# One load of the weight instead of two, held in slots, with eight mean subtractions moved to GpSimd and the rounding of the weight ranked lower, in a layernorm + banded product + fp8 linear kernel

## The chip, the cores and the metric

The kernel runs on one core of one Trainium2 chip. The metric is the time of one execution on the device, in microseconds (us). The kernel before takes 323.88 us (median of 3 runs, 323.79 to 323.97). Engines are named as in the profile: PE is TensorE (PEld its weight loads), DVE is VectorE, ACT is ScalarE, POOL is GpSimd, SP is SyncE, which issues most loads.

## The reference, cut to what matters

x is 4096 rows (8 x 512) of 1024 float32.

```
xn   = layernorm(x)                            # per row, no scale and shift
attn = einsum('ds,td->st', w1, w2) * sparse_mask
y    = gelu(xn @ attn + b2)
w_q  = fp8_e4m3(weight * (448 / max|weight|))
x_q  = fp8_e5m2(xn * (57344 / max|xn|))
z    = (x_q @ w_q.T) / x_scale / w_scale + bias
out  = x + y + z
```

Two numbers are maxima over everything: max|weight| and max|xn|. No fp8 product can start before both are known, and max|xn| needs every row of x to be normalized (or its mean taken off, and the maximum multiplied by the row's inverse deviation).

## The kernel before, in words

The rows are 32 tiles of 128 x 1024. Tiles 0 to 15 are "early": they stay in SBUF from their first load. Tiles 16 to 31 are "late": they are loaded for their statistics and maximum, dropped, and loaded again for the linear stage. sparse_mask is zero outside a band, so each 128-row piece of attn is multiplied on at most 268 columns (`band`, `band_pieces`); a check at the end, `check_mask`, looks at the rest and sets a flag, on which a general path would run.

First stage. `load_attn` brings w1, the columns of w2 and the mask for each of the eight pieces of attn (L248), `attn_matmuls` and `attn_mask` form them. For an early tile: `statistics` (DVE, L292), a root of variance for a group of tiles (`GROUPS`, by GpSimd in `inverse_root_gpsimd`, L337, for all but the first and last group), `normalize` on ScalarE for tiles 0 and 1 and `normalize_gpsimd` (L375) for the others, `row_max` (DVE, L380), eight transposes on TensorE (`transpose_one`, L462), two evictions (ScalarE, or VectorE for the second half of tiles 8 to 15), a preload of b2 into PSUM (`preload`, L483), the banded product (`product_matmul`, L487) and gelu (L497). For a late tile: tiles 16 to 23 have mean and squares taken by ScalarE (`mean_of`, `squares`), tiles 24 to 31 have statistics by VectorE and their mean taken off by ScalarE (`mean_minus`, L313); then `row_max_late` (L385).

The weight is loaded twice by `load_weight` (L257): once for its row maxima (`weight_amax`, L428), and once more to be scaled by ScalarE (`weight_scaled`, L433), given a rounding constant by VectorE (`weight_magic`, L437, two buffers), and rounded by GpSimd in two halves of two instructions each (`weight_rounded`, L446). The maxima over all rows go through two tiny transposes on TensorE (`amax_rows` to `scale_and_inverse`, L390 to L417).

Second stage. `quantize` (L516) makes fp8 tiles; the linear of each tile is interleaved on TensorE with the product of a late tile and the transposes of the next (`interleaved`). GpSimd issues DMAs that add x to the gelu of the early tiles (`add_x`, L500).

The order on every queue is set by `Plan` (L115): each step is written down with an engine, a cost in us, a rank, what it comes after, and what it takes and frees of counted resources (33 slots of 4 KB per partition in the pool "slots", PSUM buffers, "stream", "twice", "magic", "late"). The planner runs these costs forward and each time takes the ready step of lowest rank; the steps are then emitted in that order, and each engine runs its queue in order. Costs and ranks thus move no work by themselves, only its place in the queues. Loads are ranked by their place in `LOADS` (L72).

Of the kernel before, what the change touches and what calls it, by code (L numbers as in the profile page):

```python
# [26 lines left out]
STREAM = 5  # L27
# [3 lines left out]
BY_VECTOR = range(EARLY // 2, EARLY)  # L31
BY_SCALAR = range(0, 2)
GROUPS = [(0, 2), (2, 4), (4, 8), (8, 12), (12, EARLY), (EARLY, EARLY + 8), (EARLY + 8, 28), (28, 32)]
# [37 lines left out]

def load_order():  # L72

    late = iter([*SQUARED, *(i for i in range(EARLY, TILES) if i not in SQUARED)])
    early = iter(range(EARLY))
    found = [("x", next(early)), ("x", next(early))]
    for sc in range(NC):
        found += [("attn", sc)]
        found += [("x", i) for i in (next(early, None), next(early, None)) if i is not None]
        found += [("x", next(late))]  # L80
    found += [("once", c) for c in range(NC)]
    for c in range(NC):
        found += [("twice", c), ("x", next(late))]
    return found
    return found
# [90 lines left out]
def banded_path(  # L176
# [138 lines left out]

    def variance(lo, hi):
        v["var", lo] = small.tile([P, hi - lo], F32, tag="var", name=f"var_{lo}")
        nc.vector.tensor_scalar_add(v["var", lo], mean_var[:, lo:hi, 1], LN_EPS)
# [109 lines left out]
    def weight_amax(c):  # L428
        nc.vector.tensor_reduce(
            w_cols[:, c : c + 1], ws.pop(c), AX.X, ALU.max, apply_absolute_value=True  # L430
        )
# [155 lines left out]
    plan = Plan(slot=SLOTS - 1, quant=QUANT, y=4, f=2, t=2, stream=STREAM, magic=2, twice=4, late=LATE)  # L587
# [6 lines left out]
    def load(cost, emit, *args, take=(), after=()):  # L594
        op = do(LOAD, cost, len(loads), emit, *args, lag=2.0, take=take, after=after)
        loads.append(op)
        return op

    late_first = [i for i in SQUARED]
    late_rest = [i for i in range(EARLY, TILES) if i not in SQUARED]  # L600
    x_ops, attn_ops, w_once, w_twice, mask_ops = {}, {}, {}, {}, {}

    def more(kind, k):
# [4 lines left out]
        elif kind == "once":  # L608
            w_once[k] = load(1.4, load_weight, k, take=("slot", "stream"))
        else:  # L610
            w_twice[k] = load(1.4, load_weight, k, take=("slot", "twice"), after=(w_once[NC - 1],))

    for kind, k in LOADS:
        more(kind, k)

    b2_op = do(G, 0.6, 1, load_b2, lag=12.0, after=(attn_ops[0],))

    attn_mm, attn_ready = [], []
    for sc in range(NC):
        mm = do(  # L620
            T, 3.5, sc * 0.1, attn_matmuls, sc, after=[attn_ops[c] for c in range(sc + 1)],
# [4 lines left out]
            do(V, 0.42, 0, attn_mask, sc, after=(mm,), free=("f",))  # L626
# [5 lines left out]
    for i in range(TILES):  # L632
        if i in SQUARED:
            m = do(A, 1.6, 5 + 0.01 * i, mean_of, i, after=(x_ops[i],))
            stat[i] = do(A, 1.4, 4, squares, i, after=(m,))
        else:
            stat[i] = do(V, 1.43, 4 + 0.01 * i, statistics, i, after=(x_ops[i],))
    for lo, hi in GROUPS:
        group = [stat[i] for i in range(lo, hi)]
        if 0 < lo and hi < TILES:  # L640
            op = do(G, 1.7 + 0.16 * (hi - lo), 0, inverse_root_gpsimd, lo, hi, after=group)
        else:
            op = do(V, 0.2, 0, variance, lo, hi, after=group)
            op = do(G, 0.4 + 0.16 * (hi - lo), 0, power, lo, hi, after=(op,))
# [8 lines left out]
    for i in range(EARLY):  # L653
        if i in BY_SCALAR:
            normal[i] = do(A, 1.14, 3 + 0.01 * i, normalize, i, after=(shifted[i],))
        else:
            normal[i] = do(G, 1.2, 3 + 0.01 * i, normalize_gpsimd, i, after=(shifted[i],))
        maxima[i] = do(V, 1.15, 3 + 0.01 * i, row_max, i, after=(normal[i],))

        settled[i] = do("later", 0.0, i, lambda: None, lag=2.0, after=(normal[i],))  # L660
    for i in range(EARLY, TILES):
        ready = stat[i]
        if i not in SQUARED:
            ready = do(A, 1.14, 3.5, mean_minus, i, after=(ready,))
        maxima[i] = do(V, 1.15, 3 + 0.01 * i, row_max_late, i, after=(ready,), free=("slot", "stream"))
# [9 lines left out]
    def global_amax(name, fp8_max, rank, cols, after):  # L675
# [6 lines left out]
    bias_op = do(G, 0.6, 0, load_bias, lag=6.0, after=(maxima[TILES - 3],), take=("slot",))  # L682

    sums = [
        do(V, 1.15, 2, weight_amax, c, after=(w_once[c],), free=("slot", "stream")) for c in range(NC)
    ]
    w_known = global_amax("w", E4M3_MAX, 0, w_cols, sums)
    rounded = []
    for c in range(NC):
        op = do(A, 1.1, 1, weight_scaled, c, after=(w_known, w_twice[c]))  # L690
        op = do(V, 1.4, 1, weight_magic, c, after=(op,), take=("magic",))
        op = do(G, 2.55, 1, weight_rounded, c, 0, after=(op,))
        rounded.append(do(G, 2.55, 1, weight_rounded, c, 1, after=(op,), free=("slot", "magic", "twice")))
# [5 lines left out]
    for i in range(EARLY):  # L699
        in_big = i >= EARLY - NC  # L700
        for q in range(2):
# [5 lines left out]
            engine, emit = (V, evict_by_vector) if q and i in BY_VECTOR else (A, evict_transposed)  # L707
            evicted[i, q] = do(engine, 0.55, 1.5, emit, i, q, after=(op,), free=("t",))
        pre = [
            do(A, 0.55, 2 + 0.01 * i, preload, i, h, after=(b2_op,), take=("y",)) for h in range(2)  # L710
# [3 lines left out]
        for piece in band_pieces():  # L714
            op = do(
                T, 0.4, 10 * i, product_matmul, i, *piece, lag=0.1 if not piece[-1] else 0.2,
                after=(op, evicted[i, 0], attn_ready[piece[0]], pre[piece[1]]),
            )
            if piece[-1]:
                ends.append(do(A, 0.55, 0, gelu_early, i, piece[1], after=(op, maxima[i]), free=("y",)))  # L720
# [8 lines left out]
    steps = [0]  # L729
    for n in range(1, EARLY):  # L730
# [403 lines left out]
```

## Time and profile before

| what | value |
|---|---|
| median of the runs | 323.88 us |
| time of the profiled execution | 324.16 us |
| its span | 322.3 us |
| mean granted clock of TensorE | 0.987 |
| busy of PE, DVE, ACT, POOL | 290.0, 235.5, 160.9, 136.1 us |
| weight tiles loaded by SP | 16 of 512 KB |
| reads of HBM, writes | 56.60 MB, 16.78 MB |

The profile is of one execution. Starts are us from the start of the span. A row of a timeline gives start, duration, engine, line, operation, output and input, how many records it merges (two records are one float32 matmul), and in brackets how long the engine had been idle and what ended that. The table of stretches gives, for each, the time in which each engine was busy, the mean clock granted to TensorE as a share of full speed, the share of the 16 DMA engines and GB/s.

### The profile page before, as it was taken

How to read it: one execution, taken by the hardware profiler on the slowest of the kernel's cores; microseconds unless marked ns; L12 is line 12 of the kernel's file. 1: busy time of each engine (PE TensorE's matmuls, PEld its weight loads, DVE VectorE, ACT ScalarE, POOL GpSimd, SP SyncE). 2: the span in 40 equal slices, each digit the busy share in tenths (PEclk: the TensorE clock that was granted, in tenths of full speed). 3: DMA queues.
4: the chain of work that ended last, by engine and by line, in shares of the span. 5: the costliest groups of instructions: out<-in, count | busy, mean ns of one | idle time of the engine just before them, and what ended most of it. 6: DMA issues, size and time to landing. Idle time of an engine off the chain costs nothing. (4 is left out here: it accounts for less than half of the span.)

```text
span 322.3 us, 4326 instructions
## 1 busy us (share of the span) xinstructions
PE 290.0 (90%) x1526; PEld 216.9 (67%) x1545; DVE 235.5 (73%) x343; ACT 160.9 (50%) x260; POOL 136.1 (42%) x163
## 2 busy tenths in 40 slices
PE   2669879998899598999989999999999999999992
PEld 0657668887789486876756766676676667667650
DVE  3587797989999899845587677677767766766581
ACT  1467459595895879663244335344523524452110
POOL 2052608183689898996343113311311331131160
PEclk9999999999999789999999999999999999999998
DMA  7999999999607731199999999973344233121313
GB/s 255 399 370 369 380 380 379 373 409 409 254 0 251 272 130 65 11 190 255 293 292 294 305 309 306 410 274 141 120 147 179 72 128 130 75 119 68 132 66 138
DMA packets 28365, 73.74 MB, mean 229 GB/s; under 512 B 3376, under 2 KB 11568, under 8 KB 28336
## 3 DMA queue, kind: packets, MB, share of 16 engines
q1 hardware_dynamic: 20992, 47.17, 40.2%
q0 software_dynamic: 2592, 9.44, 14.2%
q10 hardware_dynamic: 4752, 16.78, 13.1%
q8 instruction: 14, 0.23, 0.3%
q14 instruction: 15, 0.12, 0.1%
HBM read 56.60 MB, written 16.78 MB: 228 GB/s over the span
## 5 line engine op out<-in xcount | busy, mean ns | idle before, releaser
L528 PE MATMUL pf<-wq,xqts 128*128 128x512 bf16 x493 | 145.5, 379 | 1.6 <-DVE x L543 1.0
L488 PE MATMUL py<-attn,xnt 128*128 128x268 f32 (+2 forms) x480 | 115.6, 341 | 2.9 <-ACT py L485 1.7
L488 PEld LDWEIGHTS py<-attn,xnt 128*128 128x128 f32 x480 | 86.3, 190 | 26.3 <-ACT py L485 2.0
L513 POOL TENSOR_TENSOR x<-x,gelu 128x512 f32<-128x512 f32 x32 | 41.2, 1287 | 110.6 <-ACT gelu L510 109.0
L540 DVE SCALAR_TENSOR_TENSOR pf<-pf,descale,bias_bc 128x512 f32<-128x512 f32 x62 | 46.9, 756 | 53.3 <-PE pf L528 50.9
L528 PEld LDWEIGHTS <-xqts 128*128 128x128 fp8e5 x512 | 50.6, 101 | 23.7 <-issue 0.2
L510 ACT ACTIVATE gelu<-py 128x512 f32<-128x512 f32 x32 | 19.1, 597 | 77.7 <-PE py L488 77.7
L543 DVE TENSOR_TENSOR x<-pf,x 128x512 f32<-128x512 f32 x62 | 42.9, 692 | 5.0 <-DMA x<-in_x_dram 1.0
L381 DVE TENSOR_REDUCE row_amax<-x 128x1 f32<-128x1024 f32 x32 | 37.9, 1206 | 6.3 <-POOL x L376 3.0
L278 PE MATMUL pa<-w_sb,w 128*128 128x268 f32 (+1 forms) x128 | 30.5, 393 | 9.6 <-DMA w_sb<-in_w2t_dram 9.5
L488 PE MATMUL py<-attn,xnt_big 128*128 128x198 f32 (+2 forms) x160 | 34.8, 364 | 4.0 <-ACT py L485 4.0
L485 ACT COPY py<-b_bc 128x512 f32<-128x512 f32 x64 | 37.3, 599 | 1.0
L295 DVE BATCH_NORM_STATS2 st<-x 128x6 f32<-128x512 f32 x48 | 30.4, 675 | 9.8 <-DMA x<-in_x_dram 9.8
L478 ACT COPY xnt<-pt 128x512 f32<-128x512 f32 x48 | 27.2, 579 | 15.4 <-PE pt L469 14.8
L278 PEld LDWEIGHTS pa<-w_sb,w 128*128 128x128 f32 x128 | 24.6, 201 | 15.1 <-issue 12.0
L469 PE MATMUL pt<-ident,xn 128*128 128x128 f32 x128 | 34.0, 273 | 0.2
L488 PEld LDWEIGHTS py<-attn,xnt_big 128*128 128x128 f32 x160 | 28.1, 205 | 7.0 <-ACT py L485 4.7
L469 PEld LDWEIGHTS pt<-ident,xn 128*128 128x128 f32 x128 | 17.8, 141 | 14.4 <-DVE xnt_big L481 0.5
L367 ACT ACTIVATE xn<-x,shift,rstd 128x1024 f32<-128x1024 f32 x16 | 19.9, 1244 | 12.0 <-DVE x L543 7.3
L521 DVE TENSOR_SCALAR xqts<-xnt,x_scale 128x1024 fp8e5<-128x1024 f32 x24 | 25.8, 1080 | 0.0
L469 PE MATMUL pt<-ident,x 128*128 128x128 f32 x128 | 19.1, 279 | 3.5 <-ACT xnt L478 1.8
L498 ACT ACTIVATE x<-py 128x512 f32<-128x512 f32 x32 | 18.3, 598 | 6.4 <-PE py L488 6.4
(86 smaller groups left out, 228.1 us busy)
## 6 DMA issues: line engine op xcount, KB each, us to landing
x<-in_x_dram SPq DMA_DIRECT2D x48, 512.0 KB, 8.0
out_dram<-x ACTq DMA_DIRECT2D x31, 512.0 KB, 3.2
w<-in_wt_dram SPq DMA_DIRECT2D x16, 512.0 KB, 8.8
x<-in_x_dram POOLq DMA_DIRECT2D x16, 512.0 KB, 25.5
w<-in_w_dram SPq DMA_DIRECT2D x8, 512.0 KB, 9.4
mask<-in_mask_dram SPq DMA_DIRECT2D x8, 512.0 KB, 9.7
w_sb<-in_w2t_dram SPq DMA_DIRECT2D x6, 512.0 KB, 10.9
attn<-in_mask_dram SPq DMA_DIRECT2D x6, 134.0 KB, 9.5
```

Of the source, the lines that this page charges most:

```text
L278: nc.tensor.matmul(pt[:, : hi - lo], w1_sb[:, c, :], w2_sb[:, c, lo:hi], start=(c == 0), stop=(c == NC - 1),)
L295: nc.vector.bn_stats(st[:, h, :], xs[i][:, half(h)])
L381: nc.vector.tensor_reduce(row_amax[:, i : i + 1], xs[i], AX.X, ALU.max, apply_absolute_value=True)
L469: nc.tensor.transpose(pts[i, q][:, j, :], xn[:, c * P : (c + 1) * P], ident)
L478: nc.scalar.copy(xnts[i][:, q * (NC // 2) : (q + 1) * (NC // 2), :], pts.pop((i, q)))
L485: nc.scalar.copy(pys[i, h], b2_bc[:, half(h)])
L488: nc.tensor.matmul(pys[i, h][:, lo - h * HALF : hi - h * HALF], xnts[i][:, sc, :], attn[:, sc, lo - band(sc)[0] : hi - band(sc)[0]], start ...
L513: nc.gpsimd.tensor_add(xs[i][:, half(h)], xs[i][:, half(h)], gelus[i][:, half(h)])
L521: nc.vector.tensor_scalar(v["quant"][:, xqts[i]], xnts.pop(i), v["x"][0], E5M2_MAX, ALU.mult, ALU.min, saturate=False)
L528: nc.tensor.matmul(v["pf", i, h], v["quant"][:, xqts[i], c, :], wq[:, c, half(h)], start=(c == 0), stop=(c == NC - 1),)
L540: nc.vector.scalar_tensor_tensor(pf, pf, v["descale"], v["bias"][:, half(h)], ALU.mult, ALU.add)
L543: nc.vector.tensor_add(res[:, half(h)], pf, res[:, half(h)])
```

## The change

The weight is loaded once. Its eight tiles stand in the load order behind the fourth of the eight pieces of attn, and keep their slots until the second half of their rounding; `stream` is 8 instead of 5, "twice" is gone. The string `ORDER` gives the loads by kind (a: attn, e: early x, o: weight, s: tiles 16 to 23, l: tiles 24 to 31); late tiles that stood between the early ones now come behind. The means of tiles 24 to 31 are taken off by GpSimd, in one tensor_scalar each. Scaling of the weight has rank 4 instead of 1, its magic 2 instead of 1, its rounding 5 instead of 1. Most costs in the plan are written anew. The order of the second stage is the same.

```diff
-STREAM = 5
+STREAM = 8
+CENTRED_BY_GPSIMD = range(24, 32)
+ORDER = (
+    "eeaeeaeeaeeaooooooooaeeaesaesaesesesesssllllllll"
+)
...
+    def mean_minus_gpsimd(i):
+        nc.gpsimd.tensor_scalar(
+            xs[i], xs[i], -1.0, mean_var[:, i, 0:1], ALU.mult, ALU.add
+        )
...
     def weight_amax(c):
         nc.vector.tensor_reduce(
-            w_cols[:, c : c + 1], ws.pop(c), AX.X, ALU.max, apply_absolute_value=True
+            w_cols[:, c : c + 1], ws[c], AX.X, ALU.max, apply_absolute_value=True
         )
...
-        elif kind == "once":
-            w_once[k] = load(1.4, load_weight, k, take=("slot", "stream"))
         else:
-            w_twice[k] = load(1.4, load_weight, k, take=("slot", "twice"), after=(w_once[NC - 1],))
+            w_ops[k] = load(1.4, load_weight, k, take=("slot",))
...
-        if i not in SQUARED:
-            ready = do(A, 1.14, 3.5, mean_minus, i, after=(ready,))
+        if i in CENTRED_BY_GPSIMD:
+            ready = do(G, 1.23, 4, mean_minus_gpsimd, i, after=(ready,))
+        elif i not in SQUARED:
+            ready = do(A, 1.18, 3.5, mean_minus, i, after=(ready,))
...
     for c in range(NC):
-        op = do(A, 1.1, 1, weight_scaled, c, after=(w_known, w_twice[c]))
-        op = do(V, 1.4, 1, weight_magic, c, after=(op,), take=("magic",))
-        op = do(G, 2.55, 1, weight_rounded, c, 0, after=(op,))
-        rounded.append(do(G, 2.55, 1, weight_rounded, c, 1, after=(op,), free=("slot", "magic", "twice")))
+        op = do(A, 1.17, 4, weight_scaled, c, after=(w_known, w_ops[c]))
+        op = do(V, 1.8, 2, weight_magic, c, after=(op,), take=("magic",))
+        op = do(G, 2.54, 5, weight_rounded, c, 0, after=(op,))
+        rounded.append(
+            do(
+                G, 2.54, 5, weight_rounded, c, 1, after=(op,),
+                free=("slot", "magic"),
+            )
+        )
```

In the changed program GpSimd's queue reads: w_0 and w_1 first halves; root of tiles 8 to 11; w_0 second half; normalize 8 to 11; w_1 second half; w_2, w_3 whole; w_4, w_5 first halves; w_4 second; root of 12 to 15; w_5 second; normalize 12 to 15; mean of 24, 25; w_6, w_7 first halves; root of 16 to 23; w_6 second; root of the squares; root of 24 to 27; mean of 26, 27; power for 28 to 31; mean of 28 to 31; w_7 second half; load of the bias; the adds of x. The slots of the weight tiles go to later loads: x_19 takes that of w_0, x_20 of w_1, x_15 of w_2, x_22 of w_3, x_26 of w_4, x_28 of w_5, and the second load of x_17 that of w_6.

## The prediction

> **What bounds the kernel now.** I read the table of busy time by stretches first, cut where the work changes kind: loads at full rate (to 86), last statistics and rounding of the weight (to 125), the path from the last row maximum to the first matmul of the fp8 linear (125 to 134.2), and the linear itself.
>
> ```profile
> core 0: us, PE busy (x) PEld busy (x) DVE busy (x) ACT busy (x) POOL busy (x), PEclk, DMA share, GB/s
> 0.00:24.00 24.00, 12.75 (x56) 9.90 (x56) 14.23 (x27) 9.53 (x16) 7.21 (x21) 1.00 0.96 342
> 24.00:62.00 38.00, 33.51 (x175) 28.03 (x176) 30.89 (x50) 24.34 (x48) 14.39 (x24) 1.00 1.07 374
> 62.00:86.00 24.00, 22.90 (x130) 20.09 (x130) 22.57 (x34) 17.65 (x31) 13.07 (x26) 1.00 1.00 399
> 86.00:110.00 24.00, 18.45 (x110) 16.22 (x109) 22.41 (x32) 19.11 (x31) 20.90 (x24) 0.98 0.47 163
> 110.00:125.00 15.00, 14.46 (x74) 12.85 (x73) 13.69 (x22) 13.14 (x21) 13.97 (x13) 0.81 0.36 129
> 125.00:134.20 9.20, 8.11 (x48) 6.82 (x49) 8.72 (x14) 7.24 (x12) 7.81 (x7) 1.00 0.01 3
> 134.20:316.20 182.00, 179.81 (x939) 122.97 (x956) 122.29 (x172) 69.91 (x108) 58.77 (x51) 1.00 0.62 194
> ```
>
> From 134.2 on TensorE is busy 179.81 of 182 us: that stage has a fixed length, and the diff changes nothing in it. Before 134.2 TensorE is busy only 110.2 of 134.2 us, GpSimd (POOL) is nearly full from 86 on, and DMA is idle half the time there. So the question is one number: when does the first linear matmul start? The timelines of VectorE and TensorE around it:
>
> ```profile
> 124.84 0.19 DVE L392 TENSOR_REDUCE x_mine<-row_amax 128x1 f32<-128x32 f32 x1
> 126.76 0.27 DVE L401 TENSOR_REDUCE x_top<-pt_x 1x1 f32<-1x128 f32 x1
> 129.32 1.73 DVE L521 TENSOR_SCALAR xqts<-xnt,x_scale 128x1024 fp8e5<-128x1024 f32 x1
> 134.22 0.38 PE L528 MATMUL pf<-wq,xqts 128*128 128x512 bf16 x1
> ```
>
> The global maximum of x is known per partition at 125.0, the first quantized tile at 131.05, yet the matmul starts at 134.22: from 128.4 on TensorE had products left to do. TensorE itself was late by 3 us, because it had waited earlier:
>
> ```profile
> 109.61 0.70 PE L488 MATMUL py<-attn,xnt_big 128*128 128x70 f32 x2 [3.97 <-ACT py L485]
> 110.95 5.85 PE L488 MATMUL py<-attn,xnt_big 128*128 128x70 f32 x18
> ```
>
> The 3.97 us wait is ScalarE's: its preload of py stood in its queue behind a scaling of the weight that waited 3.42 us for the second load of that weight. After it, 18 records took 5.85 us; the same 18 took 3.42 at 101.44: 2.4 us more, while the clock granted in 110 to 125 is 0.81.
>
> **What the change removes.** Eight loads of 0.524 MB: at the 399 GB/s of 62 to 86 that is 10.5 us of transfer. ScalarE loses eight mean subtractions (1.15 us each) and the waits for second loads; TensorE so loses the 3.97 us wait and its 2.4 us of slow clock. None of this is a gain by itself: in the new program it is no longer TensorE that is late at the start of the linear, as the next part shows.
>
> **What it adds: GpSimd's queue becomes the path.** In the changed order, GpSimd does two halves of rounding, then waits for the statistics of x_11, and from there to the last mean subtraction (x_31) it has: three roots of 4 columns, one of 8, eight normalizations, 13 halves of rounding, the root of the squares, one power, eight mean subtractions. The maximum of x_31, and with it x_scale, waits for the last of them. Prices from these rows:
>
> ```profile
> L376 POOL TENSOR_SCALAR x<-x,rstd,shift x14: 1192/1198/1204, 20.3 to 73.9; 128x1024 f32<-128x1024 f32 x14
> 96.78 1.63 DVE L441 TENSOR_SCALAR magic<-w 128x1024 int16<-128x1024 int16 x1
> 115.50 1.16 POOL L448 TENSOR_TENSOR w<-w,magic 128x512 f32<-128x512 f32 x1
> 116.74 1.17 POOL L449 TENSOR_TENSOR wq<-w,magic 128x512 bf16<-128x512 f32 x1
> 117.87 1.16 POOL L448 TENSOR_TENSOR w<-w,magic 128x512 f32<-128x512 f32 x1
> ```
>
> - A mean subtraction on GpSimd does not occur in this trace. Its bounds are the 1.15 of ScalarE's row for it (L314) and the 2.35 of one half of rounding; the nearest row is L376, the same kind of instruction on the same shape, whose 14 members lie between 1.192 and 1.204, so I take 1.19, and the upper end has no share in the range. Eight of them and eight normalizations: 19.0.
> - Rounding: a half takes 2.35 from start to start undisturbed (115.50 to 117.87 is one), up to 2.83 beside a magic of VectorE; the 14 halves before the quantization mean 2.48. 13 x 2.48 = 32.2.
> - Roots: 4 columns 3.15 (48.51 to 51.67), 8 columns 3.7 (68.98 to 72.68), squares 3.2 (81.73 to 84.9), a power 1.3 (1.02 and 1.41). 9.4 + 3.7 + 3.2 + 1.3 = 17.6.
>
> Sum 68.8 us. **Its start**: the statistics of x_11. Ahead of and with x_11 stand 19.6 MB (13 x tiles, 8 weight tiles, 7 pieces of attn). By 24 us 8.2 MB have come, then 374 GB/s: 54.4. In the trace of before, x_20 (15.1 MB in) lands at 45.4, 3.0 later than this sum gives. So 57.4, and with 1.43 of statistics 58.8. The two halves before it are no later: w_scale is known about 50, the weights' last byte (13.4 MB) being in at 40.9 by the same sum, and they need about 5 us after the first magic at 53.
>
> **Are there waits inside the 68.8?** Walking the queues by hand with those durations: x_15 may load only when w_2 is rounded (about 77), lands 3.3 later (x_0: issued 0.73, used 4.03), and its statistics end at 88, GpSimd asking for them at 89; magic_5 waits for the buffer that w_3 frees, and is 0.4 late, which I add. The others (squares of x_16 to x_23, statistics of x_24 to x_31, magics) are 3 us or more early. So the last mean subtraction ends about 128.0. The freeing of slots for the last loads (x_29 to x_31 about 105 to 108) is nowhere near the path.
>
> **From there to the linear.** VectorE must do four maxima (1.13 each) and one eviction (0.6) after the root of the last group, whose three small instructions took 2.3 us at 115.56 beside GpSimd, 0.6 at 8.05 alone. If beside: power ends 123.2, root 125.5, maxima 130.7, x_mine 131.0. If alone: 128.0 + 1.2 + 0.4 = 129.6. Middle 130.3. x_mine to the first linear matmul, with TensorE waiting: transpose 0.3, top 0.27, row 0.21 to 1.16, transpose back 0.3, scale and descale 0.8, quantize 1.1 to 1.7: 3.0 to 4.5, I take 3.7. First linear matmul at **134.0** against 134.22.
>
> TensorE: after the normalization of x_12 (about 96) it has seven products of 3.5 us, 40 transposes at 0.11 us each, so some 29 us, ends about 125 and then waits for x_mine. Thereby tile 15 is finished before the linear; in the trace of before two of its pieces (0.8 us) still come behind the first linear matmul: -0.8. This wait of 5 us can slow the clock as the one at 105.6 did; most of the slow time falls on VectorE's small instructions, I put +0.5 (bounds 0 and 2.4). The one stall inside the linear (0.99 us at 166.5, behind a VectorE/GpSimd queue of accumulating loads) may go, as the accumulating loads are issued from about 132 instead of 135.1: -0.5 (0 to -1.0).
>
> Sum against the profiled execution (324.16, span 322.3): 324.16 - 0.2 - 0.8 + 0.5 - 0.5 = 323.2. The median of the runs shown is 0.28 lower, so **322.9**.
>
> **Two rules of the Trainium skill.** The magics above show VectorE and GpSimd in each other's way. "Advanced Engine Details and Errata", VectorE Performance Modes, says that GpSimd and VectorE in a two-port mode share a port and block each other, which speaks against putting more on GpSimd; were each of the six magics after x_11 to block it for all of its undisturbed 1.07 us, an estimate from the rows gives 6.4 us instead of the 1.7 that lie in 2.48 against 2.35, and 327.6. "TensorE: Matmul & The Clock Gate", What's actually happening, has half rate after about 3.4 us of idling, until about 3.4 us of work; an estimate from it is 1.7 us lost per long wait, where this trace shows 2.4.
>
> **Rivals.**
> 1. GpSimd's queue slips (slower than before). From 86 to 135 it lost 3.4 of 49 us to waits (0.42, 1.16, 0.61, 1.16); at that share 68.8 us lose 4.7: 322.9 + 4.7 = 327.6. Each us costs one; it decides from 1.0 us on, that is when the last mean subtraction ends later than 129. For it: 60 instructions in a row with no spare time, and eight loads that wait for them. Against it: the waits of before came from second loads and from magics at two buffers; here the magics run ahead.
> 2. The queue is at its low bounds: halves at 2.35 (-1.7), root of the last group alone (-1.4), weights loaded at 409 GB/s (the slices from 65 to 80), so x_11 1.2 earlier: 318.6. TensorE's own work, done at 125, allows it.
> 3. TensorE is late after all: the weights push attn's fifth piece to about 43, and the products are crowded. It has 9 us in hand; 12 us late would give 326.
> 4. The change frees DMA without effect, as its loads are paced by slots: that is the forecast's own reading, not a case apart.
>
> **Chances.** Forecast (321.6 to 324.2) 0.42; rival 1 0.30; rival 2 0.20; rival 3 0.08. A measurement of this kernel can tell about 0.2%, 0.65 us. Faster: 0.28 of the forecast and 0.19 of rival 2, 0.47; same: 0.13, 0.03 and 0.02, 0.18; slower: 0.35. Range 319.0 to 327.3: it leaves out the far halves of rivals 1 and 2.
>
> **What would show it.** Right: GpSimd busy nearly without a break from 59 to 128, TensorE waiting some us for pt_x, first linear matmul within 1.5 us of 134. Wrong: TensorE dense up to the linear (then the path was its own), or gaps on GpSimd that name a magic, a statistic or a load; or a linear stage of other length than 182.

## The result and the profile after

The changed kernel takes **329.06 us** (median of 4 runs, 328.94 to 329.4) against 323.84 (323.37 to 323.97): 1.0166 times as long, 95% interval 1.0148 to 1.0183. The forecast was 322.9, its range ended at 327.3, and it had called faster the likeliest side.

The stretches of the changed kernel, cut as before, with the first linear matmul at 140.63:

```profile
core 0: us, PE busy (x) PEld busy (x) DVE busy (x) ACT busy (x) POOL busy (x), PEclk, DMA share, GB/s
...
62.00:86.00 24.00, 23.97 (x148) 21.84 (x147) 22.08 (x26) 22.87 (x47) 23.10 (x23) 1.00 0.43 158
86.00:110.00 24.00, 17.51 (x95) 15.69 (x95) 21.64 (x29) 15.83 (x33) 22.50 (x25) 0.86 0.48 169
110.00:125.00 15.00, 15.00 (x91) 13.85 (x89) 11.50 (x23) 10.00 (x18) 13.09 (x27) 1.00 0.46 160
125.00:140.63 15.63, 11.01 (x43) 8.41 (x42) 14.43 (x23) 8.39 (x12) 11.19 (x12) 0.69 0.47 104
140.63:322.63 182.00, 180.08 (x954) 122.42 (x952) 120.26 (x172) 68.99 (x105) 54.77 (x47) 1.00 0.61 193
```

The last row is the linear, as dense as before. All of the loss lies ahead of it: it starts 6.4 us later, and the span is only 4.8 longer (327.1), so 1.6 us came back behind the start (the one stall of TensorE in the linear of before, 0.99 us at 166.53, is gone). GpSimd is now full from 62 (23.10 of 24), the loads run at 43% of the DMA engines where they ran at 100%, and the last stretch ahead of the linear, where TensorE is busy 11.01 of 15.63 us at a clock of 0.69, is the place to look. Its timelines, GpSimd first, then VectorE:

```profile
122.85 2.24 POOL L325 TENSOR_SCALAR x<-x,mean_var 128x1024 f32<-128x1024 f32 x2
125.06 1.04 POOL L335 TENSOR_TENSOR r<-var,neg_half 128x4 f32<-128x4 f32 x1
126.09 4.41 POOL L325 TENSOR_SCALAR x<-x,mean_var 128x1024 f32<-128x1024 f32 x4
```

```profile
126.28 0.94 DVE L341 TENSOR_TENSOR t<-r 128x4 f32<-128x4 f32 x1
127.25 1.07 DVE L342 SCALAR_TENSOR_TENSOR t<-t,var 128x4 f32<-128x4 f32 x1
128.35 1.06 DVE L343 SCALAR_TENSOR_TENSOR rstd<-t,r 128x4 f32<-128x4 f32 x1
129.45 1.06 DVE L346 SCALAR_TENSOR_TENSOR shift<-mean_var,rstd 128x4 f32<-128x4 f32 x1
130.43 3.46 DVE L394 TENSOR_REDUCE row_amax<-x 128x1 f32<-128x1024 f32 x3
...
135.86 0.19 DVE L405 TENSOR_REDUCE x_mine<-row_amax 128x1 f32<-128x32 f32 x1
...
138.13 2.73 DVE L534 TENSOR_SCALAR xqts<-xnt,x_scale 128x1024 fp8e5<-128x1024 f32 x4
```

GpSimd takes the last four means off from 126.09 to 130.50, 1.10 us each. In exactly that time VectorE does four instructions on 128x4 numbers, each about 1.06 us long, and only then the row maxima that had been ready one by one. So x_mine ends 5.55 us after the last mean. And TensorE:

```profile
127.69 0.66 PE L482 MATMUL pt<-ident,xn 128*128 128x128 f32 x4 [1.10 <-ACT xn L380]
128.18 0.84 PE L501 MATMUL py<-attn,xnt_big 128*128 128x198 f32 x4
132.37 1.11 PE L482 MATMUL pt<-ident,xn 128*128 128x128 f32 x4 [3.35 <-ACT xnt L491]
...
137.36 3.47 PE L501 MATMUL py<-attn,xnt_big 128*128 128x198 f32 x8
140.63 0.62 PE L541 MATMUL pf<-wq,xqts 128*128 128x512 bf16 x1
```

It has waits of 1.10 and 3.35 us (for slots that those late maxima free), and then its last eight records take 0.43 us each, where four took 0.21 each at 128.18; the granted clock between the end of x_mine (136.05) and the first linear matmul is 0.50.

### The profile page after: what moved, and what is told of

The parts are those of the page before. It is cut to its first block, busy times and chain, and to the rows that moved or that the text cites. A ratio compares the mean times of both kernels' runs of the same rounds, so it can differ in the third digit from the quotient of the medians.

```text
span 327.1 us, 4313 instructions
## 1 busy us (share of the span) xinstructions
PE 294.4 (90%) x1545; PEld 219.9 (67%) x1545; DVE 234.0 (72%) x343; ACT 153.8 (47%) x252; POOL 145.6 (45%) x171
## 4 chain that ended last, share of the span: by engine, by line
PE 60%; DVE 12%; DMA 10%; POOL 8%; SPq 5%; issue 2%; ACT 1%; POOLq 0%; DVEq 0%
PE pf L541 34%; PE py L501 20%; PE pt L482 5%; DVE row_amax L394 4%; DMA x<-in_x_dram 4%; DMA w_sb<-in_w2t_dram 4%; SPq L263 3%; DMA w<-in_wt_dram 2%; DVE magic L454 2%; DVE magic L457 2%; POOL wq L462 2%; POOL w L461 2%; PE pa L286 1%; POOL g_r L357 1%; DVE xnt_big L494 1%
## 5 line engine op out<-in xcount | busy, mean ns | idle before, releaser
L541 PE MATMUL pf<-wq,xqts 128*128 128x512 bf16 x512 | 149.8, 379 | 0.0
L286 PEld LDWEIGHTS pa<-w_sb,w 128*128 128x128 f32 x128 | 25.4, 206 | 16.7 <-issue 13.1
L501 PE MATMUL py<-attn,xnt_big 128*128 128x198 f32 (+2 forms) x160 | 36.2, 375 | 0.0
L501 PEld LDWEIGHTS py<-attn,xnt_big 128*128 128x128 f32 x160 | 29.3, 212 | 2.5
L461 POOL TENSOR_TENSOR w<-w,magic 128x512 f32<-128x512 f32 x16 | 19.1, 1196 | 18.3 <-DVE magic L457 18.3
L482 PEld LDWEIGHTS pt<-ident,x 128*128 128x128 f32 x128 | 15.7, 147 | 11.5 <-POOL x L389 7.7
## 6 DMA issues: line engine op xcount, KB each, us to landing
attn<-in_mask_dram SPq DMA_DIRECT2D x6, 134.0 KB, 9.5
```

The source lines that it names most:

```text
L286: nc.tensor.matmul(pt[:, : hi - lo], w1_sb[:, c, :], w2_sb[:, c, lo:hi], start=(c == 0), stop=(c == NC - 1),)
L461: nc.gpsimd.tensor_add(w[:, half(h)], w[:, half(h)], magic[:, half(h)])
L482: nc.tensor.transpose(pts[i, q][:, j, :], xn[:, c * P : (c + 1) * P], ident)
L501: nc.tensor.matmul(pys[i, h][:, lo - h * HALF : hi - h * HALF], xnts[i][:, sc, :], attn[:, sc, lo - band(sc)[0] : hi - band(sc)[0]], start ...
L541: nc.tensor.matmul(v["pf", i, h], v["quant"][:, xqts[i], c, :], wq[:, c, half(h)], start=(c == 0), stop=(c == NC - 1),)
```

## The experiments

All times beside a run of the kernel before on the same chip (324.06 to 324.55 there). The theories: **T**, the path is GpSimd's queue, VectorE's tail up to x_mine, then the linear, as predicted, but with a longer tail. **A**, TensorE's own waits set the start. **B**, later **H**: the single load is the cause, as eight slots are held by weights until they are rounded. **C**, the lower rank of the rounding is the cause. In the table x_mine end, linear start and the rest of the span behind it are of the profiled execution, the time is the median. The profiled execution lies up to 1.4 us from that median.

| kernel | time | x_mine ends | linear starts | rest |
|---|---|---|---|---|
| before | 323.84 | 125.03 | 134.22 | 188.1 |
| changed | 329.06 | 136.05 | 140.63 | 186.5 |
| means on ScalarE | 331.62 | 138.60 | 142.60 | 188.0 |
| old ranks | 332.90 | 137.77 | 144.94 | 185.7 |
| single load alone | 324.97 | 132.36 | 135.98 | 187.1 |
| last root on GpSimd | 326.97 | 137.32 | 140.81 | 185.7 |
| before, means on GpSimd | 338.44 | 116.96 | 132.92 | 202.2 |
| before, lower rank | 331.10 | 116.55 | 132.14 | 197.2 |
| means on 16 columns | 323.15 | 133.06 | 136.38 | 185.4 |
| maxima first | 328.93 | 136.38 | 142.19 | 185.4 |

**The parts, one undone at a time.** Means back on ScalarE; ranks back to 1; both (the single load alone, which keeps the change's new order of loads and its new costs in the plan; no run separates these from the single load):

```diff
-CENTRED_BY_GPSIMD = range(24, 32)
+CENTRED_BY_GPSIMD = range(0)
```

```diff
-        op = do(A, 1.17, 4, weight_scaled, c, after=(w_known, w_ops[c]))
-        op = do(V, 1.8, 2, weight_magic, c, after=(op,), take=("magic",))
-        op = do(G, 2.54, 5, weight_rounded, c, 0, after=(op,))
+        op = do(A, 1.17, 1, weight_scaled, c, after=(w_known, w_ops[c]))
+        op = do(V, 1.8, 1, weight_magic, c, after=(op,), take=("magic",))
+        op = do(G, 2.54, 1, weight_rounded, c, 0, after=(op,))
```

> The changed kernel with the eight mean subtractions (tiles 24 to 31) back on ScalarE; single load and lower rank of the rounding stay. Theory T (the path is GpSimd's queue, then VectorE's tail up to x_mine, then the linear): GpSimd loses 8 x 1.11 = 8.9 us ahead of the last row maximum, so x_mine ends at 127 to 129 instead of 136.05, the first linear matmul starts at 131.5 to 133.5 instead of 140.63, and the time falls from 329 to 320-323. Rival A (TensorE's own waits, 6.49 us for the normalization of x_12 and 3.35 us for a slot, set the start): the waits stay, the start stays at 138 or later, 326-329. Rival B (the single load, whose weights hold slots until they are rounded, is the cause): 327 or more, with loads behind the rounding as they were.

> The changed kernel with the rounding (scaling, magic, halves) back at its old rank 1, so that it goes ahead of the normalizations; the means of tiles 24 to 31 stay on GpSimd and now all come after the last half of rounding. Theory T: the same instructions stand in GpSimd's queue ahead of the last mean subtraction, so its end moves by no more than 2 us either way, the small instructions of VectorE still run beside them at about 1 us each, and the time is 327.5-331. Rival C (the lower rank is what costs, as it pushes the rounding into the tail): x_mine near 130, 323-325. Rival A: normalizations later, TensorE later, 331 or more, with TensorE never waiting for x_mine.

> The single load alone: the changed kernel with the means on ScalarE and the rounding at its old rank 1. Theory T: GpSimd's queue is as long as before the change, x_mine ends at 125 to 129 and the time is 320-324. Rival B (the held slots cost): the loads of late tiles wait for the rounding, statistics come late, 327 or more. Rival C (lower rank helps): 1 us or more above the kernel with the means on ScalarE and the lower rank.

Measured: 331.62, 332.90 and 324.97 us (ratios 1.021, 1.028 and 1.0028, the last with 1.0009 to 1.0046). T missed all three: the first is 2.6 us slower than the changed kernel instead of 6 to 9 faster, the second lies above 331, the third above 324. A's 331 or more fits the second in size, but TensorE does wait there for x_mine, 1.88 us. The first one's timelines, GpSimd and VectorE:

```profile
131.25 0.20 POOL L355 TENSOR_SCALAR g_var<-mean_var 128x8 f32<-128x8 f32 x1 [5.93 <-ACT x L312]
```

```profile
125.75 0.15 DVE L341 TENSOR_TENSOR t<-r 128x4 f32<-128x4 f32 x1
...
138.20 0.18 DVE L434 TENSOR_TENSOR row_amax<-row_amax,rstd 128x16 f32<-128x16 f32 x1 [5.79 <-POOL row_amax L377]
```

GpSimd did get short (its last half of rounding ends at 113.6), but now ScalarE is the queue: it is busy 14.55 of 15 us in 110 to 125, the squares of x_23 come last (at 129.93), and two roots on GpSimd wait for them. The planner had moved the work to the next full engine. The small instruction of VectorE takes 0.15 here, with GpSimd idle. What follows: the single load costs 0.9 us by the ratio, less than B needs (327 or more); the lower rank alone adds 6.6 to it, the means on GpSimd alone 7.9, both together 4.1. So the lower rank (C) and the work on GpSimd (T) each cost when they come alone, and the two don't add; C's own forecast for the old ranks, 323 to 325, was far off.

**The same two parts in the kernel before**, each alone, weights still loaded twice: the ranks 4, 2 and 5 as in the change, or

```diff
+        if i in CENTRED_BY_GPSIMD:
+            ready = do(G, 1.23, 0.5, mean_minus_gpsimd, i, after=(ready,))
-        if i not in SQUARED:
+        elif i not in SQUARED:
```

> The kernel before, with its weights loaded twice, and only the means of tiles 24 to 31 moved to GpSimd, ahead of the rounding. Theory H (new, after the first four runs: what makes the changed kernel slow is that eight of the slots are held by the weights from about 41 us until each is rounded, so that the late tiles get their slots, and with them their squares, statistics, means and maxima, only as the rounding frees them; the means on GpSimd then only choose which queue is full): without the holding, late tiles come as before, x_mine ends by 127, but GpSimd's 8.9 us more push the last halves of rounding behind it, to about 139-141, so the linear waits for the last weights: 326-331. Theory T (GpSimd's queue alone makes the time): the same direction, the whole 8.9 us shown: 332 or more. If means on GpSimd are a gain by themselves: below 323.5.

> The kernel before, weights loaded twice and means on ScalarE, with only the ranks of scaling, magic and rounding lowered to 4, 2 and 5. If the lower rank costs by itself (rounding pushed behind x_mine, the linear waiting for weights): 327 or more. Theory H (the lower rank costs only where slots are held until the rounding): the time stays within 1.5 us of before, 322.5-325.5.

Measured: 338.44 and 331.10 us, beyond what H gave for either; T's 332 or more holds for the first, and 327 or more, for a rank that costs by itself, for the second. Both have x_mine 8 us *earlier* than before (116.96 and 116.55) and lose all of it: TensorE's products last to 132 or 133 anyway, and what GpSimd has put off comes inside the linear. First the kernel with the means, TensorE, then the one with the lower rank, VectorE and TensorE:

```profile
138.67 0.46 PE L534 MATMUL pf<-wq,xqts 128*128 128x512 bf16 x1 [2.39 <-POOL wq L455]
144.26 0.58 PE L534 MATMUL pf<-wq,xqts 128*128 128x512 bf16 x1 [4.79 <-POOL wq L455]
```

```profile
159.28 0.69 DVE L543 TENSOR_TENSOR x<-pf,x 128x512 f32<-128x512 f32 x1 [9.18 <-POOL x L513]
```

```profile
160.02 0.59 PE L528 MATMUL pf<-wq,xqts 128*128 128x512 bf16 x1 [8.44 <-DVE x L543]
```

The linear waits for rounded weights (their last half ends at 147.4 instead of 135.2), or for GpSimd's additions of gelu, which stand behind accumulating loads of x in GpSimd's queue, and these behind the rounding (issued from 139.7 instead of 135.1). In these two runs the time is lost because GpSimd's queue is not done at about the linear's start.

**How much are the means themselves?** The changed kernel in its own order, the eight mean subtractions on 16 columns:

```diff
-            xs[i], xs[i], -1.0, mean_var[:, i, 0:1], ALU.mult, ALU.add
+            xs[i][:, :16], xs[i][:, :16], -1.0, mean_var[:, i, 0:1], ALU.mult, ALU.add
```

> The changed kernel in exactly its own order on every engine; only the eight mean subtractions on GpSimd work on 16 of their 1024 columns (part of the mean subtraction is left out). That takes some 8 us out of GpSimd's queue and nothing else. Theory T (the path is GpSimd's queue, VectorE's tail, the linear): the last mean ends near 122.5 instead of 130.50, the small instructions of VectorE shrink from 1.06 to some 0.2 us, x_mine ends at 124-126 instead of 136.05 and is no longer the bound; the linear then starts when TensorE is done with its products, 131-135 instead of 140.63: 320-324. Rival A (TensorE's waits for ScalarE and slots set the start): 326 or more.

Measured: 323.15 us (ratio to before 0.9952, 0.9933 to 0.9972), 5.9 below the changed kernel: T's size, and A's 326 is out. The last mean ends at 124.94 (122.5 was expected); x_mine not at 124-126 but at 133.06, as VectorE has become the queue:

```profile
122.68 2.34 DVE L394 TENSOR_REDUCE row_amax<-x 128x1 f32<-128x1024 f32 x2 [0.63 <-POOL x L325]
124.94 1.13 DVE L341 TENSOR_TENSOR t<-r 128x4 f32<-128x4 f32 x1
126.11 0.16 DVE L342 SCALAR_TENSOR_TENSOR t<-t,var 128x4 f32<-128x4 f32 x1
126.31 1.02 DVE L343 SCALAR_TENSOR_TENSOR rstd<-t,r 128x4 f32<-128x4 f32 x1
127.36 0.16 DVE L346 SCALAR_TENSOR_TENSOR shift<-mean_var,rstd 128x4 f32<-128x4 f32 x1
127.44 3.46 DVE L394 TENSOR_REDUCE row_amax<-x 128x1 f32<-128x1024 f32 x3
```

It runs without a break from the first of these to x_mine. Two of the small instructions did not shrink to 0.2 us as expected: they now stand beside a rounding. From x_mine to the linear it is 3.32 us, with the last products at full clock:

```profile
134.15 1.84 PE L501 MATMUL py<-attn,xnt_big 128*128 128x198 f32 x8
```

**VectorE's tail.** First the last group's root made by GpSimd like the others (`if 0 < lo:`, the shifts by VectorE only `if lo == 0:`); then the root left on VectorE but behind the last four maxima:

```diff
+    op = do(V, 0.6, 0, inverse_root, lo, hi, after=(last_power, *(maxima[i] for i in range(lo, hi))))
```

> The changed kernel with the root of the last group (tiles 28 to 31) made by GpSimd as for the other groups, so that VectorE's four small instructions at 126.28 to 130.51 (0.94, 1.07, 1.06, 1.06 us) are gone. Theory T: VectorE is free for the row maxima as the means come, x_mine ends 1.5 to 2.0 us after the last mean subtraction instead of 5.55; GpSimd's queue is 1.8 us longer (root of 4 columns 3.15 for a power of 1.3), so x_mine ends 1.5 to 2.5 us earlier and the time is 326.5-327.8. Rival A (TensorE's own waits set the start): no change, 328.7-329.4. If the small instructions were not in the way at all, the longer queue would cost: 330.5-331.

> The changed kernel with VectorE's four small instructions for the last group (1 us each beside GpSimd's mean subtractions) moved behind the last four row maxima; nothing else moves ahead of x_mine. Theory T: the maxima follow the means one by one, the last ends 1.2 us after the last mean subtraction (130.5), the small ones then stand beside roundings instead of mean subtractions (0.2 each, or one of them up to 1.1), x_mine ends at 132.6-133.7 instead of 136.05, and the slot that the transposed late tile waits for comes earlier: 325.5-327. If the small instructions only fill a wait that is there anyway: 328.5-329.5.

Measured: 326.97 us (326.39 to 328.24), within T's range; and 328.93 (327.69 to 329.36), not T's 325.5-327. In both profiled executions, which are the slowest of their four, the first half of rounding starts 2.0 and 2.2 us later than in the changed kernel, ahead of anything the edits touch (below), so I compare from the last mean on. Last mean to x_mine: 5.55 us in the changed kernel, 2.61 with the root on GpSimd, 3.68 with the maxima first, where one of the small ones is still slow:

```profile
134.55 0.15 DVE L341 TENSOR_TENSOR t<-r 128x4 f32<-128x4 f32 x1
134.74 1.01 DVE L342 SCALAR_TENSOR_TENSOR t<-t,var 128x4 f32<-128x4 f32 x1
135.78 0.16 DVE L343 SCALAR_TENSOR_TENSOR rstd<-t,r 128x4 f32<-128x4 f32 x1
```

Last mean to linear: 10.13, 6.10 and 9.49. With the root on GpSimd 2.94 of the 4.03 us are gained ahead of x_mine and 1.09 behind it, where the last products keep their full clock; GpSimd's queue up to the last mean is some 2.2 us longer for it. With the maxima first, TensorE waits 1.97 and 2.42 us ahead of x_mine, has transposes and products left behind it, and does the first of these at a slow clock (six records in 2.81 us); from x_mine to the linear it is 5.81 us instead of 4.58, which takes back two thirds of the gain. So the tail costs, but its small instructions alone are not the 3 us they seem.

**Are slots the cause (H)?** A 35th slot, told to the planner or not; the tile of zeros is halved for it. Then, in the single load alone, weights 4 to 7 loaded twice and 0 to 3 held; and, in the kernel with the maxima first, the early tiles ahead of the squared ones in the order of loads.

```diff
-SLOTS = 34
+SLOTS = 35
```

```diff
-    "eeaeeaeeaeeaooooooooaeeaesaesaesesesesssllllllll"
+    "eeaeeaeeaeeaooooooooaeeaeaeaeeeessssssssllllllll"
```

> The changed kernel with one slot more, 35 for 34 (room made by halving the tile of zeros of the warm-up matmuls, which are split in two). Theory H: the late tiles' loads and the two slots that the transposed late tile waited for come earlier; in this order GpSimd's queue is full from 60 to 130 whatever the loads do, so only the waits of TensorE at 127.7 and 132.4 (1.10 and 3.35 us) with their slow clock can go: 327-328.8. Theory T: no change of x_mine, 328.5-329.5.

> The changed kernel in its own order, with a 35th slot that the planner does not know of, so only the waits for slots can change (the tile of zeros of the warm-up matmuls is halved to make room, and those matmuls are split in two). Theory T: GpSimd's queue is full whatever the loads do, x_mine stays within 0.5 us of 136; the waits of TensorE at 127.69 and 132.37 (1.10 and 3.35 us, for a slot that a row maximum frees) go, and with them the slow clock after x_mine: up to 1 us, 328-329. Rival B (the held slots are the cause by themselves): 327 or less.

> The single load alone (means on ScalarE, rounding at its old rank), with 35 slots for 34. Theory H: one more slot for the late tiles, where two or three pass through at a time while the weights are held, brings the last statistics (127.5 in the run with 34) 3-6 us earlier and the time 1-3 us down: 322-324. If slots are not what the late tiles wait for: no change, 324.7-325.3.

> The single load alone in its own order, with a 35th slot that the planner does not know of (the tile of zeros of the warm-up matmuls halved, those matmuls split in two). Theory H (late tiles wait for slots that the rounding frees): the last statistics come 1-4 us earlier than 127.5, x_mine before 131, the time 323-324.5. If their order on the engines holds them and not the slots: 324.6-325.3, last statistics within 0.5 us of 127.5.

> The single load alone, but only for weights 0 to 3; weights 4 to 7 give up their slots after their maximum and are loaded a second time between the late tiles. Theory H: four slots fewer held from 41 us on, late tiles up to 8 us earlier, x_mine at 127-129 instead of 132.4, for 2.1 MB (5 us of transfer) more: 321.5-324, below both the single load alone (324.97) and the kernel before. If the holding does not matter: 325 or more, by the second loads' waits on ScalarE.

> As the run with the maxima first, and in the order of loads the last early tiles (x_11 to x_15) go ahead of the squared ones (16 to 23), so that x_15 need not wait for a slot that a rounded weight frees. Theory H (held slots): normalizations 8 to 15 come some 10 us earlier, the wait of TensorE for x_12 (6.49 us at 93.3) and its slow clock (0.86 in 86 to 110) shrink or go; but x_mine now waits for squares that come later, and GpSimd's queue keeps its length: x_mine at 131-134, TensorE done earlier: 323-326. If TensorE's wait is not from the slots: it stays above 5 us.

Measured, in this order: 329.09, 330.42, 328.99, 326.55 (324.86 to 326.95), 328.56 and 333.00 us. None of the first four is below its kernel with 34 slots (329.06 and 324.97); the last two are 3.6 above the single load alone and 4.1 above the maxima first. T's range holds for the first, and 325 or more, for a holding that does not matter, for the fifth; the other four lie above every range given. With the slot unknown to the planner (the second) the waits of 1.10 and 3.35 us shrink to 0.15, and TensorE waits 6.16 for x_mine instead; x_mine is 2.13 later, as the last mean is, since the first half of rounding starts 2.0 later (56.52, see the last section). The slow clock does not go with the waits: the last eight records take 3.47 us as before, and from x_mine to the linear it is 5.48 us. In the single load alone the last statistics start at 127.44 with 35 slots and 127.50 with 34, which speaks for the order of VectorE's queue (14.1 of 15 us busy in 110 to 125) and against slots. These two profiles do not tell why the median is 1.6 higher: the run's times lie at 324.86 to 325.06 and at 326.45 to 326.95, and the lowest is the one profiled. With half of the weights held, ScalarE waits for second loads again and x_mine ends at 139.73; with the early tiles first TensorE's wait for x_12 goes from 6.49 to nothing, and it waits 5.48 for an eviction and 8.80 for x_mine instead. So one slot more does not help, nor four that cost second loads, and H is not shown. Whether several more slots without such loads would, was not tried.

**Towards a better version.** Weights behind a fifth piece of attn ("eeaeeaeeaeeaeeaoooooooo..."); means of 24 to 27 on GpSimd and 28 to 31 on ScalarE, with the maxima first and the squares at rank 3.2; both of these; and the kernel before, where the scalings of weights 4 and 5, which waited for second loads, are put behind the next two preloads on ScalarE:

```diff
+        for c in DELAYED:
+            ops = self.behind_preloads(ops, c)
```

> The changed kernel with one piece of attn and two tiles of x more ahead of the eight weights (weights behind five pieces). If TensorE's wait for the sixth piece and what hangs on it (w_scale, the first rounding, the start of GpSimd's queue) is part of the cost: that wait goes, normalizations 8 to 11 stand ahead of the rounding, GpSimd's queue starts without the 0.43 us gaps, the last mean ends 1-3 us earlier than 130.50: 326-328. If GpSimd's queue is merely as long as before and the weights come 4 us later: 329-331.

> The changed kernel with the means of tiles 24 to 27 on GpSimd and of 28 to 31 on ScalarE, the last group's small instructions behind the maxima, and ScalarE's squares ranked ahead of its mean subtractions (so that they don't come last as they did with all means on ScalarE). Theory T: GpSimd loses 4.4 us ahead of the last maximum, VectorE's small instructions run in 0.2 us, ScalarE takes 4.6 us more but not last; x_mine at 130-132.5, TensorE ready at about the same time: 324-326.5. If ScalarE or the late loads are the next bound: 327 or more.

> As the run with shared means, and the weights behind five pieces of attn. If the two gains add: 1-2 us below the run with shared means, 322.5-325; if the later weights push the rounding into the tail: 1 us or more above it.

> The kernel before, in its own order on every engine but ScalarE, where the scalings of weights 4 and 5 (which wait 3.42 and 0.84 us for second loads at 100.0 and 106.1) go behind the next two preloads of py. If the prediction's reading of the kernel before is right (TensorE's 3.97 us wait at 105.6, then a slow clock, make it 3 us late for the linear): that wait goes and the linear starts 2-3.5 us earlier than 134.22, at the latest end of x_mine's path: 320.5-322.5. If the two scalings are themselves on the path (magic, rounding, then the power of the last group behind it on GpSimd): x_mine ends 2-5 us later than 125.03, and the time is 324-327.

Measured: 332.21, 326.67 (325.28 to 328.67), 328.22 and 324.16 us. The weights behind five pieces start the rounding 8.6 us later (63.08) and lose 3 us: the expected gain was not there, and with shared means they lose 1.55. Sharing the means is 2.4 below the change and just above T's 324-326.5, with x_mine at 134.44 in an execution near the slowest of its ten, where the first half of rounding starts 2.1 later than in the changed kernel. It can't be told apart from the last root on GpSimd (ratios to before 1.0077 and 1.0075): both are still slower than before. The last one tells of the kernel before; it missed both of its forecasts, as the wait went without the gain and x_mine did not come later. The row of its timeline of TensorE that matters, from the fastest of its twelve executions (322.31):

```profile
124.58 0.27 PE L411 MATMUL pt_x<-ident,x_mine 128*1 128x128 f32 x1 [2.72 <-DVE x_mine L406]
```

The 3.97 us wait is gone and its slow clock too (the 18 records, now at 105.88, take 3.54 instead of 5.85; two waits of 1.07 and 1.19 come behind them), yet the linear starts at 133.62, 0.6 earlier, and x_mine itself ends 0.5 earlier there (124.51): TensorE takes its queue in order, and it stands 2.72 us before the transpose of x_mine with products up to the linear still behind it. Ratio 0.9985 (0.997 to 0.9999): by 0.5 us (0.3 by the medians) the only complete version below the kernel before, at the edge of what the measurement can tell. No version was found that clearly beats both.

## Why the prediction was wrong

- **What bounds: only the start of the linear counts.** Right in the main. Behind it the profiled executions take 185.4 to 189.0 us in every kernel, but for the two in which GpSimd puts work into it. The 0.8 and 0.5 us to be saved behind it came as 1.6.
- **"TensorE itself was late by 3 us, because it had waited earlier."** Not the whole of it. Without that wait the linear starts 0.6 us earlier, no more than x_mine comes earlier; the rest becomes a wait for x_mine.
- **GpSimd's queue becomes the path.** Right. It runs from 60.17 to 130.50, 70.3 us against 68.8 and 0.4 of waits; a mean subtraction takes 1.10 (forecast 1.19), but the eight normalizations 10.8 together (forecast 9.5), each four of them starting beside a magic (65.60 and 98.09). The start is 1.4 later than 58.8: the two halves ahead of it, which "are no later" than the statistics of x_11, were later (statistics done at 58.98, second half of rounding at 60.1, with one wait of 0.43 for a magic). Together 2.5 us: the last mean at 130.5, not 128.0.
- **"From there to the linear": the step that failed.** x_mine was put 2.3 us after the last mean; it came 5.55 after it. The linear so starts 6.6 us later than the forecast 134.0: 2.5 by the last mean, 3.25 by this step and 0.9 by the next. Against the later of the step's two cases, 131.0, x_mine's 136.05 is 5.05 more: the power ended at 126.1 instead of 123.2 (2.9, mostly GpSimd's lateness), the root took 4.23 instead of 2.3 (four small instructions, not three, each as long as the mean subtraction beside it), the maxima and eviction the rest. The middle between "beside" and "alone" was no guess between equals: the alone case needed the small instructions to run while GpSimd is idle, and its queue had four mean subtractions there. The price of 2.3 had a second flaw: it was taken beside roundings, where one of the three was not held up at all:

```profile
115.56 1.12 DVE L328 TENSOR_TENSOR t<-r 128x4 f32<-128x4 f32 x1 [0.46 <-POOL r L322]
116.71 0.16 DVE L329 SCALAR_TENSOR_TENSOR t<-t,var 128x4 f32<-128x4 f32 x1
116.91 1.02 DVE L330 SCALAR_TENSOR_TENSOR rstd<-t,r 128x4 f32<-128x4 f32 x1
```

Beside the mean subtractions none got through. That the root cost time is shown by its move to GpSimd (2.1 us less by the medians).
- **x_mine to the linear, 3.7.** It took 4.58. The first four quantized tiles were made from 138.13 on, but TensorE was not waiting as the step has it: it had its last products to do, at a granted clock of 0.50. With the means on 16 columns, at full clock, the step took 3.32. The +0.5 for the clock stood beside, so this was nearly priced.
- **"It has 9 us in hand"**, of TensorE in rival 3. It was not dense up to the end, but waited 6.49 for x_12, 1.10 and 3.35. That the two slot waits did not set the start is shown: with them gone it waited 6.16 for x_mine and the linear started no earlier. The wait for x_12 went only together with another order of loads, where TensorE waited 8.80 for x_mine.
- **Rival 1** named the right path and the wrong reason: it had GpSimd slip by waits (4.7 us), and there were two of 0.43. Its condition, the last mean later than 129, was met.
- The whole change against its parts: the single load, which has the plainest benefit (8 loads and 4.2 MB fewer), is worth nothing here (+0.9 us, with the new order of loads). That DMA was idle half the time from 86 on in the kernel before fits this, but no run shows it as the reason. Leaving out most of the means' work on GpSimd takes 5.9 us off the changed kernel, more than the net loss.

The page "Advanced Engine Details and Errata", VectorE Performance Modes, of the Trainium skill says that GpSimd and VectorE instructions in a two-port mode block each other. The trace shows such blocking, with its size: 0.15 to 0.16 us for the small ones with GpSimd idle, 1.06 beside a mean subtraction of 1.10. But the first of the four is a tensor_tensor, for which the same section lists no two-port mode, so that sentence doesn't cover it, and the trace doesn't show the mode of any. The prediction applied the rule to the magics alone, with 6 x 1.07 us as the upper end and 1.7 us in its sum; at most 3.4 us came (13 halves in 32.7 instead of 30.6, and 1.3 at the normalizations). What had no price was the blocking of the small instructions on which the path ended.

## What to carry to other kernels

When work is moved onto an engine so that its queue becomes the path, price what the *next* engine must do behind the last item, instruction by instruction in its queue order, and take every small one that runs beside the moved work at that work's length (1.06 for 0.16 us here), unless a row shows otherwise, as the row maxima do below. In this kernel, where four engines are each busy over 90% of a stretch (62 to 86), relieving one moved the bound to the next within a few us (GpSimd, ScalarE, VectorE and TensorE in turn), so look at the slack of the others for what an edit can gain, and not at its own size. A wait that is removed from an engine that works in order is a gain only if the next thing in its queue does not wait for something that comes no earlier.

## What the runs showed of the hardware that was not expected

**Small instructions in step with GpSimd.** The starts of VectorE's four 128x4 instructions lie 0.97 to 1.10 us apart, those of GpSimd's mean subtractions 1.10; row maxima beside them kept their 1.15 to 1.2. Beside roundings every other small one was held up: 1.12, 0.16, 1.02 in the kernel before, 1.13, 0.16, 1.02 with the means on 16 columns, 0.15, 1.01, 0.16 with the maxima first. The held ones end with the GpSimd instruction beside them: in the kernel before at 116.68 and 117.93, the roundings at 116.66 and 117.91. Why the mean subtractions let none through is not shown.

**An early wait that doubles.** TensorE waits about 2 us for the attn piece behind the eight weights. In the changed kernel and in the one with the maxima first, whose orders are the same up to there:

```profile
43.84 3.85 PE L286 MATMUL pa<-w_sb,w 128*128 128x268 f32 x16 [1.49 <-DMA w_sb<-in_w2t_dram]
```

```profile
44.37 5.54 PE L286 MATMUL pa<-w_sb,w 128*128 128x268 f32 x16 [2.17 <-DMA w_sb<-in_w2t_dram]
```

In the second, the granted clock is 0.60 in 46 to 50; the mask of that product stands in VectorE's queue ahead of the weight's maximum, so w_scale and the first half of rounding come 2.2 us later (56.75 instead of 54.53), and all of GpSimd's queue with them. The first half of rounding is as late with the last root on GpSimd, with shared means and with the slot unknown to the planner, each with that product in 5.26 us or more; so their x_mine is compared with the changed kernel's from the last mean on. The doubling would fit the spread between executions of one kernel (0.5 to 3.4 us in those with the single load), but only one of each was profiled, so that is not shown. The length of that wait alone doesn't decide: a run with 2.29 us kept its full clock. What does, stays open.
